# A three-layer CIN kernel: r1 picked from the gathered rows of r0, x ahead of W0 and W1 on the queue, W0's turns behind V2's spreading

## The chip, the cores and the metric

The kernel runs on one core of a Trainium2 chip. The core has a matrix engine (TensorE, PE in the profile, with its weight loads as PEld), a vector engine (VectorE, DVE), a scalar engine (ScalarE, ACT), GpSimd (POOL), a sequencer that only issues transfers (SyncE, SP), and DMA engines that all of these can give work to. Each engine runs its own instructions in the order in which they were written; between engines, semaphores order them. The metric is the time of one launch on the device, in microseconds (us); lower is better.

## The reference

The reference is a compressed interaction network. A sample has 39 fields of 64 numbers; each layer multiplies every row of the layer before with every field, elementwise, and mixes the products into 64 rows:

```python
def _cin_layer(Xk, X0, W, b):
    Wr = W.reshape(O, Hk, Fdim)
    return jnp.einsum('bhe,bfe,ohf->boe', Xk, X0, Wr) + b[None, :, None]
X0 = sparse_embedding            # (1024, 39, 64)
Xk = X0
outs = []
for W, b in ((W0, b0), (W1, b1), (W2, b2)):
    Xk = _cin_layer(Xk, X0, W, b)
    outs.append(Xk.sum(axis=-1))
return jnp.concatenate(outs, axis=-1) @ fc_w.T + fc_b
```

There are 1024 samples and three layers of 64 rows; the result is one number for each sample. All of it is f32.

## The kernel before

**The mathematics.** Only sums of the layers reach the result, so the last layers can be folded into weights: W2 with the last part of fc_w gives a small matrix V2, and W1 with V2 gives a second set of weights beside W0. The kernel then needs, for each column (a sample and one of its 64 places), two quadratic forms of the 39 fields, 64 rows of each. They are one matmul: the products of all pairs of fields, times weights for the 128 rows (wa). One form plus its bias times the other is summed over the 64 places, and the rest is linear.

**Blocks and steps.** The samples are worked in blocks of 32, which are 2048 columns. `load` copies a block's x into a table in DRAM (xd, with a row for each field, and a row of ones written by `fill_ones`). From the table GpSimd gathers rows by lists of row numbers (`roll`, `gather_rows`, L146) into tiles of 128 rows (r0 for the first block, r1 for the second, with five tiles each: rt[0][:, 0] to rt[0][:, 4]). VectorE multiplies two such tiles (`product`, L202): that is a step's product p, 128 pairs by 2048 columns. PE multiplies it with the step's weights (`multiply`, L551), 128 x 512 columns at a time, in two passes for f32, so 8 passes for a step. Four products can be in flight (the pool prods). Six steps and a smaller one (`join`, from the tiles u and v) make the whole of a first block. Later blocks are worked in another form with 32-row pieces (L763), which the change doesn't touch.

**The head.** Before the first step everything has to be made: the lists of rows (small VectorE operations from iotas and constants), a unit matrix, and the weights. The order is that of the code, since the kernel writes each engine's order by hand:

- ScalarE issues the loads of w2s, w0s, x of the first block, and w1s, in this order on one queue; SyncE those of fcrow and the ones.
- PE turns the last part of fc_w into a column, makes V2 from w2s (L378, a VectorE transpose, L419 which spreads it, VectorE's L427), turns W0 (`turn_w0`, L388, seven transposes, which ScalarE copies into the tile both, L479), and multiplies W1 with V2 (`product_v2`, L450). VectorE transposes that (L459), and ScalarE and VectorE copy it into both (`keep_group`, L467 and L470).
- `weight_rows(c)` adds the two halves of both for the pairs of step c (L510, into pairs), `weight_turn(c)` transposes them on PE (L527), and ScalarE copies them to wa (L528, L529).
- The first product needs tiles 0 and 1 of r0. Tile 1 is not waited for: its rows are those of tile 0 in another order. `pick` is a 0/1 matrix with this order, picked its transpose, and four matmuls (L910) pick the rows into four PSUM banks called r1, from which VectorE multiplies (L925). What they pick from is xs: the first block's x, read back from the table by SyncE into 39 rows, with the first 1024 columns at row 0 and the others at row 64 (L243). Its first load waits until w1s has landed.
- `spin` issues matmuls on constants (L261) whose result nobody reads: dummies, 256 columns in two passes each, unless told otherwise. There are some at the start, one behind the pick, five ahead of product_v2, and two and three behind r1, around the first weight turn.

GpSimd issues the gathers of r0 in the order 0, 2, 3, 1, 4, then u and v, then r1's five, then the loads of the second pair of blocks. x of the second block is loaded by SyncE (`load(1, product=...)`), which waits for r0's first gather. Step n's product needs tiles (0, 1), (0, 2), (3, 2), (3, 1), (0, 4), (3, 4) in this order.

Of the kernel before, what the change touches and what calls it, by code (L numbers as in the profile page):

```python
# [16 lines left out]
FT = F + 1  # L17
# [23 lines left out]
NY = 3  # L41
# [73 lines left out]
def cin_kernel(ctx: ExitStack, tc: tile.TileContext, x, w0t, b0, w1, b1, w2, b2, fc_w, fc_b, out):  # L115
# [13 lines left out]
    def bank(name):  # L129
        return psum.tile([128, MM], F32, name=name, tag="po")  # L130
# [14 lines left out]
    def gather_rows(dst, table, k, product=None):  # L145
        work = nc.gpsimd.indirect_dma_start(  # L146
            dst, None, table, bass.IndirectOffsetOnAxis(ap=lists[:, k : k + 1], axis=0)
        )
        behind(work, product)
        return work  # L150
# [37 lines left out]
    xs = ut[1]  # L188
# [19 lines left out]
    with prep as prep:  # L208
# [29 lines left out]
        nc.scalar.dma_start(w2s, w2.rearrange("o (s n) -> (o s) n", s=2))  # L238
        nc.scalar.dma_start(w0s, w0t.rearrange("b (s a) h -> (b s) (a h)", s=NW))
        load(0, nc.scalar)  # L240
        behind_w1 = nc.scalar.dma_start(w1s, w1.rearrange("o (s n) -> (o s) n", s=2))
        for k in range(2):
            work = nc.sync.dma_start(  # L243
                xs[H * k : H * k + F].rearrange("f (k c) -> f k c", c=128),
                xd[0][0:F, bass.ts(k, SUB)].rearrange("f (k c) -> f k c", c=128),
            )
            behind(work, behind_w1)
# [11 lines left out]
        def spin(n=1, cols=MM // 2, to=idle):  # L259
            for _ in range(n):  # L260
                nc.tensor.matmul(  # L261
                    to[:, MM - cols :],
                    nc.const_aps.tensor(1.0, (128, 128), F32),
                    nc.const_aps.tensor(1.0, (128, cols), F32),
                    start=True,
                    stop=True,
                )
# [99 lines left out]
        for h in (0, H):  # L367
            nc.vector.tensor_scalar(pick[:, h : h + F], apart[:, 0:F], seats, None, ALU.is_equal)
        nc.vector.memset(wfin[0:H], 1.0)
        load(1, product=gather_rows(rt[0][:, 0], xd[0][:FT], 0))  # L370
# [41 lines left out]
        for k in range(7):  # L412
            turn_w0(k)
# [71 lines left out]

        for h in (0, H):
            turn_row(h, 1, fcrow, 0)
        turn_row(0, 2, fcrow, 2)
        spin(5)
        for k, a in groups:  # L490
            product_v2(k, a)
# [28 lines left out]
    def weight_turn(c, tr=None):  # L520
        place = len(turned) % 4 * 128
        if place:
            tr = turned[-1]
        elif tr is None:
            tr = bank("tr")
        turned.append(tr)
        nc.tensor.transpose(tr[:, place : place + 128], pairs[:, c], unit)  # L527
        nc.scalar.copy(wa[:, c, 0 : 2 * H], tr[:, place : place + 2 * H])  # L528
        nc.scalar.copy(wa[:, c, 2 * H :], tr[:, place : place + H])  # L529
# [378 lines left out]
    for m in (0, 2, 1, 3):  # L908
        rows = slice(m // 2 * H, m // 2 * H + F)
        nc.tensor.matmul(r1[m], picked[rows], xs[rows, fine[m % 2]], start=True, stop=True)  # L910
    weight_rows(0)
    tr = bank("tr")
    open_block(0)
    spin(2, to=po[0][1])
    weight_turn(0, tr)
    spin(3, to=po[0][1])
# [23 lines left out]
    def whole_step(at, n, c):  # L940
        if at == NPAIR - 1:
            nc.scalar.copy(ones1, ones)
            fill_ones(1, nc.sync, ones1)
            nc.sync.dma_start(b0s, b0.rearrange("(o h) -> o h", o=1).to_broadcast([2, H]))
# [69 lines left out]
    def late_words():  # L1014
        nc.sync.dma_start(b1s, b1.rearrange("(h o) -> h o", o=1).to_broadcast([H, 2]))
        nc.gpsimd.dma_start(b2s, b2.rearrange("(h o) -> h o", o=1))
        nc.gpsimd.dma_start(fcb, fc_b.rearrange("(p o) -> p o", o=1).to_broadcast([NY * 32, 1]))
# [119 lines left out]
```

## Time and profile before

| | |
|---|---|
| median of 3 runs | 738.67 us |
| the runs | 738.67, 741.1, 738.58 us |
| time of the profiled execution | 740.52 us |
| its span, first to last instruction | 738.7 us |
| mean granted PE clock of the span | 0.993 |
| DMA moved | 153.56 MB, mean 208 GB/s |

The profile comes from one execution, which ran by itself and has its own time; times in it count from its first instruction. A row of the timeline gives start and length in us, the engine (with a q for its sequencer, which issues transfers and waits), the line, the operation, the tiles as out<-in, the shapes, how many instructions the row merges, and in brackets how long the engine stood idle before it and what ended that. A row of the chain of waits gives start, length and what the end was waiting for. The granted clock is the share of PE's full clock that was allowed in a stretch.

### The profile page before, as it was taken

Reading aid. Unit: us, or ns where it says so; the run is one execution under the profiler, and the core shown is the slowest. Engines: PE = TensorE matmul, PEld = TensorE weight load, DVE = VectorE, ACT = ScalarE, POOL = GpSimd, SP = SyncE. Lnnn points to the kernel's source line nnn. Section 1 sums busy time; section 2 is a strip of 40 time slices with the busy share of each in tenths; the row PEclk is TensorE's granted clock in tenths of the full one; section 3 lists DMA queues with packets and bytes.
Section 4 is the critical chain, followed back from the end, with each engine's and each line's share of the span. In section 5 each row is a group of like instructions: output and inputs, shape, how many; then the busy total and the mean of one; then the engine's idle time right before and its main releaser. Section 6 shows DMA issues by size and latency. Waiting matters only on the chain.

```text
span 738.7 us, 13824 instructions
## 1 busy us (share of the span) xinstructions
PE 732.6 (99%) x5961; PEld 341.5 (46%) x5961; DVE 636.8 (86%) x566; ACT 114.8 (16%) x199; POOL 522.3 (71%) x287
## 2 busy tenths in 40 slices
PE   8999999999999999999999999999999999999998
PEld 5544444444444444444444444444444444444443
DVE  5979889689797988979889797988979889797996
ACT  3242111020110202011020110202011020200322
POOL 4458887459778697886969778697886869776200
PEclk9899999999999999999999999999999999999999
DMA  7799899752946648284672937548284672855600
GB/s 272 253 333 400 327 275 337 218 177 75 303 140 217 218 124 293 88 279 164 187 273 67 319 119 235 201 133 290 83 294 152 195 261 78 292 188 178 279 0 0
DMA packets 73515, 153.56 MB, mean 208 GB/s; under 512 B 40262, under 2 KB 40347, under 8 KB 69614
## 3 DMA queue, kind: packets, MB, share of 16 engines
q0 software_dynamic: 31936, 131.34, 50.3%
q1 hardware_dynamic: 39833, 19.36, 10.8%
q10 hardware_dynamic: 1685, 1.99, 0.8%
q8 instruction: 46, 0.75, 0.4%
q14 instruction: 15, 0.12, 0.1%
HBM read 150.54 MB, written 10.28 MB: 218 GB/s over the span
## 4 chain that ended last, share of the span: by engine, by line
PE 97%; DMA 2%; ACTq 0%; DVE 0%; ACT 0%; issue 0%; DVEq 0%; SPq 0%
PE po L763 76%; PE po L551 17%; PE po L776 2%; DMA w1s<-in_w 1%; PE po L571 1%; DMA u<-xd 1%; PE po L261 1%; PE r L910 0%; PE po L582 0%; PE idle L910 0%; PE tr L527 0%; ACTq L139 0%; DVE g L827 0%; PE po L691 0%; DVE sums L859 0%; ACT z L825 0%
## 5 line engine op out<-in xcount | busy, mean ns | idle before, releaser
L763 PE MATMUL po<-p,wc 32*128 32x512 f32 x1300 | 561.9, 588 | 0.0
L763 PE MATMUL po<-p,wn 32*128 32x512 f32 x3900 | 561.7, 588 | 0.0
L719 POOL DMA_INDIRECT r<-xd,narrow x130 | 371.9, 2861 | 102.1 <-DVE p L736 69.9
L763 PEld LDWEIGHTS po<-p,wn 32*128 32x128 f32 x3900 | 260.7, 185 | 209.8 <-issue 209.8
L763 PEld LDWEIGHTS po<-p,wc 32*128 32x128 f32 x1300 | 239.4, 185 | 86.6 <-issue 81.7
L736 DVE TENSOR_TENSOR p<-r 128x2048 f32<-128x2048 f32 x78 | 176.1, 2283 | 8.2 <-PE po L763 7.8
L825 ACT ACTIVATE z<-po,columns 64x512 f32<-64x512 f32 x128 | 87.4, 683 | 542.9 <-PE po L763 503.6
L736 DVE TENSOR_TENSOR p<-r,u 128x2048 f32<-128x2048 f32 x52 | 118.6, 2282 | 16.2 <-PE po L763 15.1
L551 PE MATMUL po<-p,wa 128*128 128x512 f32 x288 | 126.2, 596 | 0.0
L202 DVE TENSOR_TENSOR p<-r 128x2048 f32<-128x2048 f32 (+2 forms) x41 | 79.9, 1973 | 10.2 <-PE po L551 9.4
L146 POOL DMA_INDIRECT r<-xd,lists x30 | 65.5, 2183 | 31.1 <-DVE p L736 11.6
L551 PEld LDWEIGHTS po<-p,wa 128*128 128x128 f32 x288 | 54.2, 191 | 68.5 <-issue 61.6
L736 DVE TENSOR_TENSOR p<-r,v 128x2048 f32<-128x2048 f32 x26 | 59.7, 2296 | 25.0 <-PE po L763 25.0
L827 DVE SCALAR_TENSOR_TENSOR g<-po,b0s,z 64x512 f32<-64x512 f32 x76 | 56.9, 749 | 5.8 <-ACT z L825 3.5
L719 POOL DMA_INDIRECT v<-xd,narrow x26 | 37.5, 1444 | 9.1 <-issue 7.6
L827 DVE SCALAR_TENSOR_TENSOR pairs<-po,b0s,z 64x512 f32<-64x512 f32 x26 | 19.5, 749 | 23.9 <-ACT z L825 23.5
L719 POOL DMA_INDIRECT u<-xd,narrow x26 | 28.7, 1103 | 9.5 <-DVE pairs L827 3.4
L809 DVE TENSOR_REDUCE sums<-g 103x16 f32<-103x1024 f32 x26 | 31.3, 1204 | 0.0
L827 DVE SCALAR_TENSOR_TENSOR both<-po,b0s,z 64x512 f32<-64x512 f32 x26 | 19.5, 749 | 0.8
L730 DVE TENSOR_TENSOR p<-u,v 128x1024 f32<-128x1024 f32 x13 | 15.7, 1208 | 1.1 <-PE po L763 1.1
L820 ACT COPY g<-r 39x1024 f32<-39x1024 f32 x12 | 12.1, 1042 | 28.9 <-DVE sums L848 15.6
L809 DVE TENSOR_REDUCE sums<-pairs 103x16 f32<-103x1024 f32 x13 | 15.7, 1205 | 0.0
(161 smaller groups left out, 192.0 us busy)
## 6 DMA issues: line engine op xcount, KB each, us to landing
xd<-in_x SPq DMA_DIRECT2D x27, 312.0 KB
g<-xd SPq DMA_DIRECT2D x26, 156.0 KB
r<-xd,narrow POOLq DMA_INDIRECT x130, 6.3
pairs<-xd SPq DMA_DIRECT2D x13, 156.0 KB
both<-xd SPq DMA_DIRECT2D x13, 156.0 KB
wn<-wc SPq DMA_DIRECT2D x12, 168.0 KB
xd<-in_x POOLq DMA_DIRECT2D x4, 312.0 KB, 8.1
w2s<-in_w ACTq DMA_DIRECT2D x1, 624.0 KB
```

Source lines behind the costliest of these rows:

```text
L146: work = nc.gpsimd.indirect_dma_start(dst, None, table, bass.IndirectOffsetOnAxis(ap=lists[:, k : k + 1], axis=0))
L202: nc.vector.tensor_tensor(p[:, cols], r[:, i, cols], r[:, k, cols], ALU.mult)
L551: nc.tensor.matmul(po[n][m], wa[:, c, side : side + 2 * H], p[:, bass.ts(m, MM)], start=n % 2 == 0 and c == 0, stop=n % 2 == 1 and c == NP ...
L719: work = nc.gpsimd.indirect_dma_start(slot(k, j), None, table, bass.IndirectOffsetOnAxis(ap=narrow[:, j : j + 1], axis=0),)
L730: done = nc.vector.tensor_tensor(p[:, 0:SUB], slot(k, LEFT), slot(k, RIGHT + NK), ALU.mult)
L736: done = nc.vector.tensor_tensor(p.rearrange("p (k c) -> p k c", k=NK), slots(k, many, NK, side), slot(k, one)[:, bass.ts(side, MM)].unsqu ...
L763: nc.tensor.matmul(po[2 * k + side][s], weights(c, s)[:, kind : kind + 2 * H], p[rows, bass.ts(u, MM)], start=begin, stop=last and u == le ...
L776: nc.tensor.matmul(po[2 * k + side][s][half : half + H], weights(LINEAR, s)[:, H : 2 * H], slot(k, NK)[rows, bass.ts(side, MM)], start=Fal ...
L809: nc.vector.tensor_reduce(sums[:, at : at + BB].rearrange("p (h s b) -> p h s b", h=2, s=2)[:, :, side], g[k, side, b].rearrange("p (h b e ...
L820: nc.scalar.copy(gt[H : H + F], tiles_of(n)[0:F, 0, bass.ts(m, SUB)])
L825: nc.scalar.activation(z[one], po[n][m][other], AF.Identity, bias=fc0s[other])
L827: return lambda: nc.vector.scalar_tensor_tensor(gt[0:H, at], po[n][m][one], b0s[one], z[one], ALU.add, ALU.mult)
```

## The change

1. The four r1 matmuls pick from the rows of r0's tile 0 itself, the gathered rows 0 to 38 and 64 to 102, instead of from xs; reading x back into xs goes. Rows 64 to 102 hold the fields in another order (25 to 38, then 0 to 24), so the second half of pick is written in two pieces.
2. On ScalarE's queue x comes ahead of w0s and w1s.
3. The second block's x is loaded by GpSimd, behind the first gather and ahead of the other four, no longer by SyncE with a wait for the gather.
4. W0's turns come behind the spreading of V2 on PE; the three fc turns come behind product_v2.
5. The dummies: one between spreading and W0's turns, two ahead of product_v2, one and a half behind the fc turns; none behind r1. With them go `spin`'s and `weight_turn`'s extra arguments and the early opening of the first block's banks.
6. b0 is loaded in two transfers of 64 rows instead of one; b2 and fc_b by SyncE instead of GpSimd, late in the kernel.

```diff
-        nc.scalar.dma_start(w0s, w0t.rearrange("b (s a) h -> (b s) (a h)", s=NW))
         load(0, nc.scalar)
-        behind_w1 = nc.scalar.dma_start(w1s, w1.rearrange("o (s n) -> (o s) n", s=2))
-        for k in range(2):
-            work = nc.sync.dma_start(
-                xs[H * k : H * k + F].rearrange("f (k c) -> f k c", c=128),
-                xd[0][0:F, bass.ts(k, SUB)].rearrange("f (k c) -> f k c", c=128),
-            )
-            behind(work, behind_w1)
+        nc.scalar.dma_start(w0s, w0t.rearrange("b (s a) h -> (b s) (a h)", s=NW))
+        nc.scalar.dma_start(w1s, w1.rearrange("o (s n) -> (o s) n", s=2))
...
-        for h in (0, H):
-            nc.vector.tensor_scalar(pick[:, h : h + F], apart[:, 0:F], seats, None, ALU.is_equal)
+        for at, f0, n in ((0, 0, F), (H, H % F, F - H % F), (H + F - H % F, 0, H % F)):
+            nc.vector.tensor_scalar(
+                pick[:, at : at + n], apart[:, f0 : f0 + n], seats, None, ALU.is_equal
+            )
...
-        load(1, product=gather_rows(rt[0][:, 0], xd[0][:FT], 0))
+        roll(0, (0,))
+        load(1, nc.gpsimd)
         roll(0, (2, 3, 1, 4))
...
-        for k in range(7):
-            turn_w0(k)
         spread_to = (*pt[:2], pv[1], small)
...
+        spin()
+        for k in range(7):
+            turn_w0(k)
+        spin(2)
+        for k, a in groups:
+            product_v2(k, a)
         for h in (0, H):
             turn_row(h, 1, fcrow, 0)
         turn_row(0, 2, fcrow, 2)
-        spin(5)
-        for k, a in groups:
-            product_v2(k, a)
+        spin()
+        spin(1, MM // 4)
...
     r1 = [idle] + [bank("r1") for _ in range(3)]
-    for m in (0, 2, 1, 3):
-        rows = slice(m // 2 * H, m // 2 * H + F)
-        nc.tensor.matmul(r1[m], picked[rows], xs[rows, fine[m % 2]], start=True, stop=True)
+    for m in range(4):
+        rows = slice(m % 2 * H, m % 2 * H + F)
+        nc.tensor.matmul(r1[m], picked[rows], rt[0][rows, 0, fine[m]], start=True, stop=True)
     weight_rows(0)
-    tr = bank("tr")
-    open_block(0)
-    spin(2, to=po[0][1])
-    weight_turn(0, tr)
-    spin(3, to=po[0][1])
+    weight_turn(0)
...
-            nc.sync.dma_start(b0s, b0.rearrange("(o h) -> o h", o=1).to_broadcast([2, H]))
+            for h in (0, H):
+                nc.sync.dma_start(b0s[h : h + H], b0.rearrange("(h o) -> h o", o=1))
...
-        nc.gpsimd.dma_start(b2s, b2.rearrange("(h o) -> h o", o=1))
-        nc.gpsimd.dma_start(fcb, fc_b.rearrange("(p o) -> p o", o=1).to_broadcast([NY * 32, 1]))
+        nc.sync.dma_start(b2s, b2.rearrange("(h o) -> h o", o=1))
+        nc.sync.dma_start(fcb, fc_b.rearrange("(p o) -> p o", o=1).to_broadcast([NY * 32, 1]))
```

Line numbers move by some lines with this: L910 of before is L908 of the changed kernel, L551 is L549, L450 is L443, L388 is L383, L261 is L253.

What the edits make of PE's order is seen at two places. The first is the head, from the dummy behind the pick to W1's product; idle is the dummies' bank, pw W0's turns, pt and pv the banks of V2 and of W1's product. Before:

```order
L261 MATMUL idle<-const-float32-1.0 128x256
L388 MATMUL pw<-unit,w0s 128x117 x6
L388 MATMUL pw<-unit,w0s 64x117
L419 MATMUL pt<-blocks,twice 64x11 x4
L419 MATMUL pv<-blocks,twice 64x10 x2
L419 MATMUL small<-blocks,twice 64x7 x2
L317 MATMUL small<-ones,fcrow 64x1 x3
L261 MATMUL idle<-const-float32-1.0 128x256 x5
L450 MATMUL pt<-w1s,v_73 128x320 x2
L450 MATMUL pv<-w1s,v_73 128x320 x2
```

PE's order at the same place in the changed kernel, on to the first r1 matmul:

```order
L253 MATMUL idle<-const-float32-1.0 128x256
L412 MATMUL pt<-blocks,twice 64x11 x4
L412 MATMUL pv<-blocks,twice 64x10 x2
L412 MATMUL small<-blocks,twice 64x7 x2
L253 MATMUL idle<-const-float32-1.0 128x256
L383 MATMUL pw<-unit,w0s 128x117 x6
L383 MATMUL pw<-unit,w0s 64x117
L253 MATMUL idle<-const-float32-1.0 128x256 x2
L443 MATMUL pt<-w1s,v_73 128x320 x2
L443 MATMUL pv<-w1s,v_73 128x320 x2
L309 MATMUL small<-ones,fcrow 64x1 x3
L253 MATMUL idle<-const-float32-1.0 128x256
```

W0's turns have moved behind the spreading, three of the five dummies are gone from ahead of W1's product, and the fc turns stand behind it. The second place on PE is from r1 to the first step; r_34x are the r1 banks, po the first block's, tr the turned weights. Before:

```order
L910 MATMUL idle<-u_90,picked 128x512
L910 MATMUL r_342<-u_90,picked 128x512
L910 MATMUL r_341<-u_90,picked 128x512
L910 MATMUL r_343<-u_90,picked 128x512
L261 MATMUL po<-const-float32-1.0 128x256 x2
L527 MATMUL tr<-unit,pairs 128x128
L261 MATMUL po<-const-float32-1.0 128x256 x3
L551 MATMUL po<-p,wa 128x512 x3
```

The same place on PE in the changed kernel:

```order
L908 MATMUL idle<-r_86,picked 128x512
L908 MATMUL r_340<-r_86,picked 128x512
L908 MATMUL r_341<-r_86,picked 128x512
L908 MATMUL r_342<-r_86,picked 128x512
L525 MATMUL tr<-unit,pairs 128x128
L549 MATMUL po<-p,wa 128x512 x3
```

The five dummies are gone, and the operand is the gathered tile r0 (r_86) in place of xs, which lay in the tile u. The third place is GpSimd's queue behind its last constant; r_86 is r0, r_87 the second block's r1, u_89 and v_91 the small tiles, xd_68 the first table. Before:

```order
L332 MEMSET shift_of 128x1 x14
L146 DMA r_86<-xd_68,lists 128x2048 x5
L146 DMA u_89<-xd_68,lists 128x1024
L146 DMA v_91<-xd_68,lists 128x1024
L146 DMA r_87<-xd_68,lists 128x2048 x5
L139 DMA xd_69<-in_x 1248x1x64 x2
```

The same place on GpSimd in the changed kernel:

```order
L324 MEMSET shift_of 128x1 x14
L146 DMA r_86<-xd_68,lists 128x2048
L139 DMA xd_68<-in_x 1248x1x64
L146 DMA r_86<-xd_68,lists 128x2048 x4
L146 DMA u_89<-xd_68,lists 128x1024
L146 DMA v_91<-xd_68,lists 128x1024
L146 DMA r_87<-xd_68,lists 128x2048 x5
L139 DMA xd_69<-in_x 1248x1x64 x2
```

One load stands between the first gather and the other four.

More of the change, by code (lines that the diff above doesn't have):

```diff
@@ L149, in gather_rows @@
         behind(work, product)
-        return work
     def tiles_of(n):
@@ L186, in cin_kernel @@
     vt = [const.tile([128, SUB], F32, name=f"v{k}") for k in range(2)]
-    xs = ut[1]
     ones = const.tile([16, 2, 128], F32, name="ones")
@@ L238, in cin_kernel @@
         nc.scalar.dma_start(w2s, w2.rearrange("o (s n) -> (o s) n", s=2))
+        load(0, nc.scalar)
         nc.scalar.dma_start(w0s, w0t.rearrange("b (s a) h -> (b s) (a h)", s=NW))
-        load(0, nc.scalar)
-        behind_w1 = nc.scalar.dma_start(w1s, w1.rearrange("o (s n) -> (o s) n", s=2))
-        for k in range(2):
-            work = nc.sync.dma_start(
-                xs[H * k : H * k + F].rearrange("f (k c) -> f k c", c=128),
-                xd[0][0:F, bass.ts(k, SUB)].rearrange("f (k c) -> f k c", c=128),
-            )
-            behind(work, behind_w1)
+        nc.scalar.dma_start(w1s, w1.rearrange("o (s n) -> (o s) n", s=2))
         nc.gpsimd.iota(place, pattern=[[0, 1]], base=0, channel_multiplier=1)
@@ L256, in cin_kernel, with spin @@
         idle = bank("idle")
-        def spin(n=1, cols=MM // 2, to=idle):
+        def spin(n=1, cols=MM // 2):
             for _ in range(n):
                 nc.tensor.matmul(
-                    to[:, MM - cols :],
+                    idle[:, 0:cols],
                     nc.const_aps.tensor(1.0, (128, 128), F32),
@@ L518, in cin_kernel, with weight_turn @@
     turned = []
-    def weight_turn(c, tr=None):
+    def weight_turn(c):
         place = len(turned) % 4 * 128
-        if place:
+        if not place:
+            tr = bank("tr")
+        else:
             tr = turned[-1]
-        elif tr is None:
-            tr = bank("tr")
         turned.append(tr)
@@ L907, in cin_kernel @@
     r1 = [idle] + [bank("r1") for _ in range(3)]
-    for m in (0, 2, 1, 3):
-        rows = slice(m // 2 * H, m // 2 * H + F)
-        nc.tensor.matmul(r1[m], picked[rows], xs[rows, fine[m % 2]], start=True, stop=True)
+    for m in range(4):
+        rows = slice(m % 2 * H, m % 2 * H + F)
+        nc.tensor.matmul(r1[m], picked[rows], rt[0][rows, 0, fine[m]], start=True, stop=True)
     weight_rows(0)
-    tr = bank("tr")
-    open_block(0)
-    spin(2, to=po[0][1])
-    weight_turn(0, tr)
-    spin(3, to=po[0][1])
+    weight_turn(0)
     for k, (n, c) in enumerate(steps[:AHEAD]):
```

## The prediction, as it was made before the run

> **What bounds the kernel now.** First the page: engine totals, the granted clock, the chain that ended last.
>
> ```profile
> PE 732.6 (99%) x5961; PEld 341.5 (46%) x5961; DVE 636.8 (86%) x566; ACT 114.8 (16%) x199; POOL 522.3 (71%) x287
> PEclk9899999999999999999999999999999999999999
> PE 97%; DMA 2%; ACTq 0%; DVE 0%; ACT 0%; issue 0%; DVEq 0%; SPq 0%
> ```
>
> TensorE (PE) is 97% of the chain: what it has to multiply is fixed, and only time in which it does nothing useful can go. The change touches only the head of the program, so the second view is the chain of waits over the first 45 us (start, length, what).
>
> ```profile
> 2.86 6.49 DMA w1s<-in_w
> ...
> 9.43 5.36 DMA u<-xd
> ...
> 14.84 1.81 PE idle L910 x2
> 16.65 3.09 PE r L910 x6
> 19.74 2.00 PE po L261 x4
> 21.74 0.21 PE tr L527
> 21.96 2.56 PE po L261 x6
> 24.52 3.07 PE po L551 x6
> 27.59 0.11 PE tr L527
> 27.69 3.44 PE po L551 x8
> ```
>
> The end is set, in order, by the landing of w1s at 9.35, the reading back of xs (u), the four r1 matmuls (L910), the dummies (L261), and from 24.5 the main matmuls (L551) without a break: 3.44 us for a step's 8 passes and 0.11 for a weight turn, a pass of 512 columns being 0.43. The third view gives the granted clock by stretches (the columns after the window: its length, busy time of PE, PEld, DVE, ACT, POOL with counts, clock, DMA share, GB/s).
>
> ```profile
> 13.20:14.80 1.60, 0.00 (x0) 0.00 (x0) 1.44 (x7) 1.24 (x4) 0.94 (x1) 1.00 0.98 218
> 15.43:25.67 10.24, 10.24 (x21) 5.76 (x20) 7.96 (x29) 0.58 (x4) 0.00 (x0) 0.51 0.99 398
> 25.70:40.00 14.30, 14.30 (x38) 6.43 (x37) 12.00 (x41) 3.83 (x12) 10.92 (x6) 1.00 0.62 206
> ```
>
> PE stands still for 1.6 us until u lands, and then runs 10.24 us at half the clock, almost exactly the stretch in which r1, the dummies and the first main passes lie. So the head pays three times: for the wait, for the clock, and for dummies run at that clock.
>
> ```profile
> 24.31 1.06 PE L551 MATMUL po<-p,wa 128*128 128x512 f32 x1
> ```
>
> The main stream starts at 24.31, in the tail of the half clock: its first six passes take 3.07 us of the chain instead of 6 x 0.43 = 2.58. At full clock it would have had to begin at **24.8** to stand where it stands. The working is about how far this point moves.
>
> **The change part by part.** *x ahead of W0, r1 from r0.* The wait of L910 is now for the first gather r0 instead of for u.
>
> ```profile
> 2.00:4.00 2.00, 2.00 (x9) 1.82 (x9) 1.80 (x13) 0.00 (x1) 1.87 (x30) 1.00 0.85 304
> w0s<-in_w0t ACTq DMA_DIRECT2D x1, 380.2 KB
> L146 POOLq EVENT_SEMAPHORE  x1: 43/43/43, 7.2 to 7.2; - x1
> 8.06 1.20 POOL L146 DMA_INDIRECT r<-xd,lists  x1 [3.96 <-DVE v L427]
> 13.90 0.97 SPq L139 DMA_DIRECT2D xd<-in_x  x1
> ```
>
> GpSimd's wait for x ends at 7.2 and the gather starts at 8.06 (the VectorE operation that its row names comes behind that and is none that it reads). SyncE's load of the second block waits for r0 and starts at 13.90, so r0 takes 5.8 us from start to landing. With x ahead, the 380.2 KB of w0s no longer pass before it: 1.2 us at 304 GB/s. r0 then starts at 6.85 and lands at about 12.7. W1 still follows W0 and x on the same queue, so it lands near 9.35 again; r0's data begins behind it. Bounds: 12.3, if nothing of w1s is in its way, to 13.9, if the saving is lost to it; I take 12.7. L908 starts there, 2.1 us before 14.84.
>
> *W0's turns, fewer dummies ahead of W1.* Can PE, VectorE and ScalarE be ready by then?
>
> ```profile
> 6.49 0.86 PE L388 MATMUL pw<-unit,w0s 117*128 117x117 f32 x7
> 8.42 2.44 PE L261 MATMUL idle<-const-float32-1.0 128*128 128x256 f32 x10
> 10.70 1.32 PE L450 MATMUL pt<-w1s,v 128*128 128x320 f32 x4
> 11.86 1.32 PE L450 MATMUL pv<-w1s,v 128*128 128x320 f32 x4
> 11.48 1.09 DVE L459 STREAM_TRANSPOSE flat<-pt 128x320 f32<-128x320 f32 x2 [2.65 <-PE pt L450]
> 7.09 1.93 ACT L479 COPY both<-pw 64x468 f32<-64x468 f32 x4 [0.50 <-PE pw L388]
> 13.77 0.45 DVE L467 COPY both<-flat 64x288 f32<-64x288 f32 x1
> 14.33 0.65 DVE L510 TENSOR_TENSOR pairs<-both 128x4 f32<-128x4 f32 x6
> ```
>
> Five dummies held PE until 10.70 although w1s was there at 9.35. Now two stand ahead of it, and W0's seven turns (0.86 us) run while w1s is awaited: w0s was there by 6.49 and now has x's 312 KB ahead of it, 1.0 us at 304 GB/s, so 7.5 at the latest, and the turns and two dummies end by 9.3. So product_v2 runs 9.4 to 11.9, 1.3 earlier; the three fc turns and two dummies (256 and 128 columns, four passes, 0.65 us) fill PE to about 12.6. VectorE's transposes, the copies and weight_rows(0) follow 1.3 earlier, done at 13.7 instead of 14.98. ScalarE's copies of W0 end near 10 instead of 9.02, ahead of VectorE's first transpose at 10.2, which its next ones need: hidden. One pick operation more is 0.1 to 0.2 us on VectorE before 5.5, hidden behind the wait for w2s and x. Moving b2s and fcb to SyncE and splitting b0s lies hundreds or tens of us from where they are read: zero.
>
> *r1 at full clock.* With PE idle for under half a us ahead of L908 I expect no drop. L910 took 4.90 us at mostly half clock; half of it is 2.45, the low end; 8 passes of 0.43 one after another, 3.44, the high end. I take 2.5, since the row groups alternate as before: done at 15.2, the first bank at 13.7.
>
> *The dummies behind r1.* Four and six passes, 2.00 and 2.56 us, leave the chain. What is late next is the turn of the first weights and ScalarE's two copies of it.
>
> ```profile
> 21.99 0.27 ACT L528 COPY wa<-tr 128x128 f32<-128x128 f32 x1 [7.42 <-PE tr L527]
> 22.16 0.22 ACT L529 COPY wa<-tr 128x64 f32<-128x64 f32 x1
> 18.39 1.28 DVE L925 TENSOR_TENSOR p<-r,r 128x512 f32<-128x512 f32 x2 [1.02 <-PE r L910]
> 20.96 2.42 DVE L202 TENSOR_TENSOR p<-r 128x512 f32<-128x512 f32 x3
> 24.28 2.42 DVE L202 TENSOR_TENSOR p<-r 128x512 f32<-128x512 f32 x3
> 30.63 2.27 DVE L202 TENSOR_TENSOR p<-r 128x2048 f32<-128x2048 f32 x1
> ```
>
> Turn at 15.1, copies done at 15.8 (0.38 from 21.99 to the end of the second), first main matmul at **15.8**. VectorE's quarters run from 13.75, one each 0.64: the first is ready at 14.4. Does VectorE keep ahead? Its spacing in these rows is p1 2.57 behind the second quarter, p2 3.32 later, p4 6.35 after p2. So p1 starts at 16.9, p2 at 20.2, p4 at 26.6, done at 28.9; PE's fifth step, four times 3.55 after 15.8, wants p4 at 30.0. It holds, with 1.1 us to spare where there were 6.1 before (32.9 against 24.8 and the same 14.2): the lead that hid VectorE is nearly spent, and from there it grows again.
>
> *The second block's x by GpSimd.* This is what can spend the rest.
>
> ```profile
> 9.56 0.94 POOL L146 DMA_INDIRECT r<-xd,lists  x1 [0.30 <-issue]
> 27.30 0.94 POOL L146 DMA_INDIRECT u<-xd,lists  x1 [13.07 <-DVE p L202]
> 41.00 2.07 POOL L139 DMA_DIRECT2D xd<-in_x  x2
> xd<-in_x POOLq DMA_DIRECT2D x2, 312.0 KB, 9.7
> ```
>
> Issuing a load on GpSimd takes 1.0 us (2.07 for two), with 0.3 of gap. r0 ends its issue at 8.05, so the next gather issues at 9.4 instead of 9.56: not later. Its data, 312 KB, now stands ahead of r2's in the same queue, 0.8 us at the 398 GB/s above; a gather's megabyte is 2.6 us. r2 lands near 16.1, r3 18.7, tile 1 21.3, tile 4 24.0, against needs of 16.9, 20.2, 23.5 and 26.6. u's gather, held until 27.30 because SyncE's load lands late, is free at 14.4; the gathers behind it move up by as much, so nothing later starves. What the load costs is bounded by nothing and by its 9.7 us to landing; I take 0.8, from the rate.
>
> The Trainium skill speaks against this step: "DMA: Bandwidth & Descriptors", section "Issuing engine by pattern", gives simple loads to Sync and calls that path generally faster. The trace does not agree here: GpSimd's loads land 9.7 after issue under load, SyncE's kept u waiting over 13. By the rule the second rival below would be likelier.
>
> **The sum**, against the profiled execution: L908 starts 2.1 earlier; r1 takes 2.4 less; the dummies' 4.56 go and 0.5 of waiting comes, 4.0; the first passes at full clock, 0.5. Together 9.0, or 24.8 to 15.8. That execution took 740.52 (span 738.7), so **731.5**. It took 1.85 longer than the median of the runs shown, 738.67; I take that for the half-clock stretch, which need not cost the same in each execution, and since I expect none, I count from the profiled one. Counted from the median it would be 729.7. I say 731.6.
>
> **The rivals.** *The clock drops all the same.* L910 uses 39 of 128 rows, and PE stayed at half clock right through it; if such matmuls count as little work, L908 and the 0.5 us wait behind it look like the gap of before, and the dummies that followed are gone. A stretch of 10.24 at half clock behind 15.8 costs 5.1: 736.6; if dense matmuls end it after a third, 733.2. For it speaks the row at 15.43; against it, that PE has no standstill of 1.6 us any more.
>
> The Trainium skill, "TensorE: Matmul & The Clock Gate", section "Why this matters for your kernels", asks only that no idle gap exceed about 3 us; here 1.6 us was enough, so the measurement decides. By its rule neither kernel would drop, and the new time would be the forecast. Its Part 1 says that the activity window is 3413 ns and free-running; three of them are the 10.24 seen here, which the trace bears out, and its phase would differ between executions.
>
> *The load ahead of r2 costs its worst.* If it lands 8 us after issue, at 16.2, then r2 lands at 19, p1 is 2.4 late and p4 1.4 behind PE: 733.0. The long times to landing speak for it, but those were taken with other gathers in the queue.
>
> *r0 does not land earlier*, because W0 and W1 now run beside it: L908 at 13.9, 1.2 lost, 732.8. So the reordering would not do what it says; the rest would.
>
> *Slower.* The clock drops twice in a row: ScalarE's copies, VectorE's thin lead and the missing dummies leave holes in the first steps, and every hold of 10.24 brings the next. Each costs 5.1, so from the second on, 10.2 exceeds the 9.0 won: 741.7. Against it: from 25.7 the trace shows not one drop in a stream of the same steps.
>
> **How the numbers follow.** Forecast 0.56; clock drop 0.26; load ahead of r2 0.08; r0 not earlier 0.06; slower 0.04. The range reaches from the count from the median, with L908 at its early end (729.2), to the full drop (736.8); only the slower rival and odd phases lie outside. About 0.5% is what a measurement of this kernel can tell from no change: 735.0 to 742.4 is then "the same". The forecast, the load, r0 and a third of the clock drop lie below 735.0, 0.78; the rest of the drop and part of the slower rival are the same, 0.19; 0.03 are above.
>
> **What would show it.** Right: L908 at 12.7 directly behind the dummies, a granted clock of 1.00 through 10 to 30, first main matmul near 15.8, no PE idle before p4. Wrong: a clock near 0.5 anywhere between 12 and 26; VectorE's p1 released by the gather of r; L443 released by w1s well after 9.4; any PE idle in the first five steps.

## The result, and the profile after

The changed kernel took 732.50 us (median of 6 runs, 732.12 to 733.14), the kernel before 738.66 (median of 6, 738.57 to 741.1): a ratio of 0.991, interval 0.9895 to 0.9923. The forecast was 731.6, with a range of 729.2 to 736.8. The profiled execution of the changed kernel took 732.4, its span 730.6. On another chip its median was 736.84 against 739.34 (e11 below).

The page of the changed kernel, engine totals, granted clock and shares of the chain:

```profile
PE 725.8 (99%) x5951; PEld 336.7 (46%) x5951; DVE 636.7 (87%) x567; ACT 114.9 (16%) x199; POOL 528.1 (72%) x286
PEclk9999999999999999999999999999999999999999
PE 98%; DMA 1%; ACTq 0%; DVE 0%; ACT 0%; issue 0%; DVEq 0%
```

PE is busy for 6.8 us less than the 732.6 of before, and the one slice with an 8 in its clock is gone. The chain of waits over the changed kernel's first 45 us (start, length, what):

```profile
2.66 6.04 DMA w0s<-in_w0t
...
8.74 0.92 PE pw L383 x7
9.66 0.88 PE idle L253 x4
10.54 1.23 PE pt L443 x4
11.77 1.16 PE pv L443 x4
...
14.10 0.62 PE idle L908
...
15.15 0.86 PE r L908 x5
16.01 0.27 PE tr L525
16.31 0.28 ACT wa L526
...
16.63 2.84 PE po L549 x6
```

The end is no longer set by w1s and u but by w0s, which lands at 8.69, three us later than the 5.69 of before; from there PE works almost without a break, at full clock, until the main stream starts at 16.63 instead of 24.31. VectorE's products in the timeline of the changed kernel (in brackets the idle time before a row and what ended it):

```profile
18.60 2.43 DVE L200 TENSOR_TENSOR p<-r 128x512 f32<-128x512 f32 x3 [0.16 <-DMA r<-xd,lists]
...
28.23 2.28 DVE L200 TENSOR_TENSOR p<-r 128x2048 f32<-128x2048 f32 x1
...
35.23 2.27 DVE L200 TENSOR_TENSOR p<-r 128x2048 f32<-128x2048 f32 x1
```

The last row is the second block's first product. Before, the same product came behind a wait (timeline of VectorE, kernel before):

```profile
41.76 2.29 DVE L202 TENSOR_TENSOR p<-r 128x2048 f32<-128x2048 f32 x1 [4.06 <-PE po L551]
```

The row names PE, but the second block's tile 1 landed at 41.57: this product waited for its data. GpSimd's gathers tell why it no longer does (timeline of GpSimd, changed kernel):

```profile
7.43 1.18 POOL L146 DMA_INDIRECT r<-xd,lists  x1 [3.54 <-DVE blocks L404]
8.62 1.07 POOL L139 DMA_DIRECT2D xd<-in_x  x1
...
16.87 0.94 POOL L146 DMA_INDIRECT u<-xd,lists  x1 [2.13 <-DVE p L919]
```

The gather of u starts at 16.87 where it started at 27.30, and what is queued behind it comes earlier too: the second block's tile 1 lands at 33.55 instead of 41.57.

For all that follows a span is cut in three: from the start to the first main matmul, from there to the first matmul of the part stage (the 32-row form of the later blocks), and from there to the end. In the two profiled executions:

| kernel | first main matmul at | main to part | part to end | span |
|---|---|---|---|---|
| before | 24.31 | 90.49 | 623.93 | 738.7 |
| changed | 16.63 | 90.06 | 623.93 | 730.6 |

The whole difference of 8.1 lies ahead of the first main matmul (7.68) and in the tail of the half clock behind it (0.43). The medians differ by 6.2 only, because the profiled execution of before was 1.85 above its median.

### The profile page after: what moved, and what is told of

It is laid out like the page before. It is cut to its first block, busy times and chain, and to the rows that moved or that the text cites. A ratio compares the mean times of both kernels' runs of the same rounds, so it can differ in the third digit from the quotient of the medians.

```text
span 730.6 us, 13801 instructions
## 1 busy us (share of the span) xinstructions
PE 725.8 (99%) x5951; PEld 336.7 (46%) x5951; DVE 636.7 (87%) x567; ACT 114.9 (16%) x199; POOL 528.1 (72%) x286
## 4 chain that ended last, share of the span: by engine, by line
PE 98%; DMA 1%; ACTq 0%; DVE 0%; ACT 0%; issue 0%; DVEq 0%
PE po L761 77%; PE po L549 17%; PE po L774 2%; DMA w0s<-in_w0t 1%; PE po L569 1%; PE po L580 0%; PE idle L253 0%; ACTq L139 0%; PE pt L443 0%; PE pv L443 0%; PE tr L525 0%; PE idle L908 0%; PE pw L383 0%; PE r L908 0%; DVE g L825 0%; PE po L689 0%
## 5 line engine op out<-in xcount | busy, mean ns | idle before, releaser
L549 PE MATMUL po<-p,wa 128*128 128x512 f32 x288 | 125.8, 594 | 0.4 <-ACT wa L526 0.4
L146 POOL DMA_INDIRECT r<-xd,lists x30 | 70.2, 2338 | 31.4 <-DVE p L734 11.6
L549 PEld LDWEIGHTS po<-p,wa 128*128 128x128 f32 x288 | 53.7, 190 | 68.6 <-issue 62.0
L825 DVE SCALAR_TENSOR_TENSOR pairs<-po,b0s,z 64x512 f32<-64x512 f32 x26 | 19.5, 749 | 23.9 <-ACT z L823 23.5
L825 DVE SCALAR_TENSOR_TENSOR both<-po,b0s,z 64x512 f32<-64x512 f32 x26 | 19.5, 749 | 0.8
L807 DVE TENSOR_REDUCE sums<-both 103x16 f32<-103x1024 f32 x13 | 15.7, 1205 | 0.0
```

The lines of the kernel that those rows point to most:

```text
L146: work = nc.gpsimd.indirect_dma_start(dst, None, table, bass.IndirectOffsetOnAxis(ap=lists[:, k : k + 1], axis=0))
L549: nc.tensor.matmul(po[n][m], wa[:, c, side : side + 2 * H], p[:, bass.ts(m, MM)], start=n % 2 == 0 and c == 0, stop=n % 2 == 1 and c == NP ...
L807: nc.vector.tensor_reduce(sums[:, at : at + BB].rearrange("p (h s b) -> p h s b", h=2, s=2)[:, :, side], g[k, side, b].rearrange("p (h b e ...
L825: return lambda: nc.vector.scalar_tensor_tensor(gt[0:H, at], po[n][m][one], b0s[one], z[one], ALU.add, ALU.mult)
```

## The experiments

The first four ran together on one chip, with 29 runs of the kernel before beside them (median 739.48); the next four (before: 738.97) and the last four (before: 739.34) on another. Each head below names the kernel that was edited; the lines with + and - are the edit.

**e1: the kernel before, its gap filled.** Does the half clock carry the loss?

```diff
         for k, a in groups:
             product_v2(k, a)
+        spin(4)
```

> The kernel before, with four dummies (8 passes, about 1.75 us) behind product_v2, where PE stood still until u landed; nothing else. Theory (the standstill of 1.6 us takes the clock): the granted clock stays 1.00 from 7 us on, the r1 matmuls take 2.0 to 2.5 us in place of 4.9, the ten dummy passes behind them 2.2 in place of 4.6, the first main matmul starts at 19.5 to 20.5 in place of 24.3, and the time falls by 2.5 to 4.5 us to 734.2 to 736.2. Rival (matmuls of 39 rows count as idle and take the clock themselves): the clock drops to 0.50 for 10.24 us all the same and the time stays at 738 to 740.

Measured: 741.1 (738.22 to 743.99, 12 runs), ratio 1.0015 [0.9999, 1.0031]. Its rows of PE's timeline, and its clock by stretches (length; busy time and counts of PE, PEld, DVE, ACT, POOL; clock; DMA share; GB/s):

```profile
16.50 1.95 PE L911 MATMUL r<-u,picked 39*128 39x512 f32 x6 [0.71 <-DMA u<-xd]
70.19 19.12 PE L552 MATMUL po<-p,wa 128*128 128x512 f32 x44 [1.96 <-DVE p L202]
```

```profile
18.57:21.99 3.42, 3.42 (x9) 2.64 (x9) 3.42 (x13) 0.58 (x4) 0.00 (x0) 0.50 1.00 413
```

The clock part came in part: not full clock, as the theory had it, but 3.4 us at half clock instead of 10.24, behind the 0.71 that PE still waited for u. The main stream began at 22.45 (its first matmul), 1.9 earlier, where 19.5 to 20.5 was expected. The time did not follow: PE then stood for 1.96 at 68.2, for the second block's products, and the part stage lost 1.4 more. So an earlier head alone buys nothing. Neither theory had that.

**e2: the kernel before, without the dummies behind r1.**

```diff
-    spin(2, to=po[0][1])
     weight_turn(0, tr)
-    spin(3, to=po[0][1])
```

> The kernel before without the five dummies behind r1; nothing else. Theory as the prediction added it up (each term by itself): the 4.6 us of dummies less 0.5 of waiting leave the head, time 734.6. Rival (the half-clock stretch is of fixed length, so main passes take the dummies' place in it at half speed): the first main matmul starts near 20.3, but the stretch runs on to 25.4, and the gain is half of what the stretch still holds, 1.5 to 2.5 us: 736.2 to 737.2.

Measured: 739.73 (739.08 to 743.87, 12), ratio 1.0007 [0.9993, 1.0022]: none of the gain. The first main matmul came at 18.40, 5.9 earlier than before, but main to part took 94.18 instead of 90.49, and part to end 625.77 instead of 623.93. The chains of waits show where it went, first e2's, then the changed kernel's:

```profile
18.40 5.38 PE po L551 x6
...
112.66 12.34 PE po L763 x96
```

```profile
106.76 10.51 PE po L761 x96
```

Some of it is the half clock, as this run's rival had it: the stretch ran from 16.71 to 23.54, now under main passes, and the first six took 5.38 where they had taken 3.07 before. PE then waited 0.8 in two places for VectorE at the second block's products, and the first 96 matmuls of the part stage took 1.83 longer than in the changed kernel, at full clock; what slows these isn't shown. So about 2 of the 5.9 went to the clock, and the rest was given back behind it.

**e3: the changed kernel with the old order of the loads** (W0 ahead of x).

```diff
+        nc.scalar.dma_start(w0s, w0t.rearrange("b (s a) h -> (b s) (a h)", s=NW))
         load(0, nc.scalar)
-        nc.scalar.dma_start(w0s, w0t.rearrange("b (s a) h -> (b s) (a h)", s=NW))
```

> The changed kernel with w0s ahead of x again on ScalarE's queue; nothing else. Theory as predicted (r0's landing sets r1, x ahead of W0 is worth 1.2 us): L908 starts 0.6 to 1.2 later, 733.1 to 733.7. Rival (PE sets it: W1's landing, its product and the dummies behind it): w0s lands near 5.7 and w1s near 9.4, PE is ready for L908 by 13.3, r0 lands near 13.9, L908 starts at 13.9 to 14.1 as now, and the time is within 0.3 of 732.5.

Measured: 732.07 (731.93 to 733.65, 5), ratio 0.9902 [0.9886, 0.9917]. From its chain of waits:

```profile
7.57 0.36 DVE v L420 x3
...
7.98 5.45 DMA r<-xd,lists
13.43 0.04 issue
13.47 0.69 PE idle L908
```

r0 landed at 13.43; with x ahead it landed at 13.40. In this pair x's place on the queue moves nothing at r0. (Over all the traces r0 landed from 12.47 to 15.14 with x ahead and from 13.34 to 15.33 with W0 ahead, so a small gain would not be seen.) With W0 first PE's work ahead of r1 is done in time, so that L908 starts at 13.47 instead of 14.03, which neither the theory nor the rival had.

**e4: the changed kernel with the second block's x by SyncE,** as before.

```diff
-        roll(0, (0,))
-        load(1, nc.gpsimd)
+        load(1, product=gather_rows(rt[0][:, 0], xd[0][:FT], 0))
```

> The changed kernel with the second block's x loaded by SyncE behind the landing of r0's first gather, as before; nothing else. Theory as predicted (the load costs r2 under 1 us that PE doesn't feel, and otherwise changes nothing that PE waits for): r2 lands 1 to 2 us earlier, p1 starts near 18, time within 0.3 of 732.5. Rival (the load by SyncE lands near 26, holds GpSimd's gather of u and with it the second block's tiles): u is gathered at 27 in place of 16.9, the second block's first product waits for its tile until 40 or later in place of 35.2, PE stands idle 1 to 4 us at 41 and the time is 733.5 to 736.5.

Measured: 739.45 (737.34 to 740.61, 12), ratio 0.9997 [0.9987, 1.0008]. The whole gain is gone with this one edit. VectorE's second block and PE's waits in its timeline:

```profile
43.49 2.29 DVE L201 TENSOR_TENSOR p<-r 128x2048 f32<-128x2048 f32 x1 [5.99 <-DMA r<-xd,lists]
```

```profile
15.19 0.69 PE L908 MATMUL idle<-r,picked 39*128 39x512 f32 x1 [0.54 <-DMA r<-xd,lists]
17.86 4.54 PE L549 MATMUL po<-p,wa 128*128 128x512 f32 x6 [0.36 <-ACT wa L526]
45.83 3.70 PE L549 MATMUL po<-p,wa 128*128 128x512 f32 x8 [1.88 <-DVE lane_of L596]
49.70 17.53 PE L549 MATMUL po<-p,wa 128*128 128x512 f32 x40 [0.17 <-DVE p L201]
68.00 19.12 PE L549 MATMUL po<-p,wa 128*128 128x512 f32 x44 [0.77 <-DVE p L201]
```

The load, issued at 15.16, sent its first data at 19.6 and its last at 26.0; u's gather started at 27.09; the second block's first product at 43.49, 8.3 later than in the changed kernel. PE waits 2.82 for it in three places, the first 96 matmuls of the part stage take 1.37 more, and a stretch of 3.4 at half clock behind the 0.54 at L908 costs some 1.7. The main stream also began 1.2 later than in the changed kernel, since r0 landed at 15.14 in this execution. So of the 8.2 between the two spans about 2.9 are the head and the clock. The one run of e4 with a mean clock of 0.999 took 737.34, 4.8 above the changed kernel; that is nearer to what the late second block costs by itself. The rival of this run was right in kind; its worst was 4.

**e5: the kernel before with only that edit,** the second block's x by GpSimd.

```diff
-        load(1, product=gather_rows(rt[0][:, 0], xd[0][:FT], 0))
+        roll(0, (0,))
+        load(1, nc.gpsimd)
```

> The kernel before with the second block's x loaded by GpSimd behind r0's first gather, and nothing else of the change. Theory (two walls: PE's head and the tiles of the second block; either alone holds the end): PE's head is as before, with the standstill and the half clock, u is gathered near 18 in place of 27, VectorE's wait ahead of the second block's first product goes, and the time stays within 1 us of before, 738.5 to 740. Rival (the second block's tiles alone set the end): the time falls to 733 to 736.

Measured: 735.83 (734.94 to 739.07, 10), ratio 0.996 [0.9943, 0.9977]: about half the gain, with the old head. The theory of two walls that each hold the end by themselves missed; the number lies in the rival's range. Its gather of u (timeline of GpSimd):

```profile
17.24 0.94 POOL L146 DMA_INDIRECT u<-xd,lists  x1 [1.94 <-DMA xd<-in_x]
```

Main to part takes 90.15 here, although its profiled execution had 6.8 us of half clock, nearly all of it ahead of the main stream. That execution's span is only 1.5 below the span of before. The four runs with a mean clock of 0.999 or more have spans of 733.1 to 733.8, so most of the gain comes from executions in which the clock drops little.

**e6: dummies behind r1 in the changed kernel.** They write into the bank of the first r1 matmul, so the first quarter of the first product is made from the dummies' result instead of the picked rows, and waits for them.

```diff
+    spin(2)
     weight_turn(0)
+    spin(3)
```

> The changed kernel with five dummies put back behind r1, two ahead of the first weight turn and three behind it, into the bank idle; nothing else. Theory (at full clock the ten passes cost 0.22 each, less the half us of waiting that they fill): first main matmul 1.7 to 2.2 later than 16.6, time 734.0 to 734.7. As the prediction priced them (4.56 at half clock): 736.5 or more. Rival (VectorE sets the start anyway): within 0.3 of 732.5.

Measured: 736.24 (734.98 to 742.07, 12), ratio 0.9972 [0.9954, 0.999]. Since VectorE is made to wait for the dummies, this doesn't price them; e10 does.

**e7: the changed kernel without the one and a half dummies ahead of r1.**

```diff
-        spin()
-        spin(1, MM // 4)
```

> The changed kernel without the one and a half dummies that stand between the fc turns and the r1 matmuls; nothing else. Theory (PE, not r0's landing at 13.40, held L908 until 14.03): L908 at 13.45, first main matmul at 16.1, clock stays 1.00, time 731.9 to 732.2. Rival (without them the stretch around r1 holds too little work and the clock drops as in the kernel before): a stretch at 0.50 of 3.4 to 10.2 us behind 13.7, time 733.5 to 737.

Measured: 733.81 (732.95 to 734.59, 6), ratio 0.9933 [0.9916, 0.9949]. The timeline of PE:

```profile
9.79 1.62 PE L383 MATMUL pw<-unit,w0s 117*128 117x117 f32 x7 [1.90 <-DMA w0s<-in_w0t]
```

A drop came, from 9.35 to 12.76, but not where the dummies had been: PE stood for 1.90 ahead of W0's turns, because w0s landed at 9.74. This run says little on the dummies and a lot on W0.

**e8: the kernel before with three edits,** GpSimd's load, the filled gap, and no dummies behind r1; it still reads x back into xs.

```diff
-        load(1, product=gather_rows(rt[0][:, 0], xd[0][:FT], 0))
+        roll(0, (0,))
+        load(1, nc.gpsimd)
...
+        spin(4)
...
-    spin(2, to=po[0][1])
     weight_turn(0, tr)
-    spin(3, to=po[0][1])
```

> The kernel before with three edits: the second block's x by GpSimd, four dummies behind product_v2, none behind r1. r1 is still picked from x read back, in the old order of loads. Theory (the second wall gone, what is left is the head): u lands at 14.8 to 16.4, r1 ends at 17 to 18.5, first main matmul at 17.6 to 19, time 733.5 to 735.5, so that picking from r0 itself is worth 1 to 3 us. Rival (the clock drops as it did with the gap filled, and PE pays half of 3.4 to 10.2 us more): 735.5 to 739.

Measured: 734.34 (733.63 to 736.36, 6), ratio 0.9948 [0.993, 0.9966], as expected. Full clock throughout, first main matmul at 18.05, main to part 90.06. From its chain of waits:

```profile
14.88 1.05 PE idle L912 x2
15.93 1.50 PE r L912 x6
...
18.05 2.84 PE po L553 x6
```

So what is left of the change, picking from r0's rows with the head's new order, is worth the rest: 18.05 against 16.63 for the changed kernel, 1.4 by the profiled executions. The medians don't settle it: e8 is 1.8 above the changed kernel's first runs, and 2.5 below its runs on e8's own chip (e11).

**e9: the changed kernel without its dummies behind V2's spreading.**

```diff
-        spin()
         for k in range(7):
             turn_w0(k)
-        spin(2)
         for k, a in groups:
             product_v2(k, a)
...
-        spin()
-        spin(1, MM // 4)
```

> The changed kernel without any of its dummies behind V2's spreading: not the one ahead of W0's turns, the two ahead of W1's product, nor the one and a half ahead of r1; nothing else. Theory (the dummies hold the clock): with PE idle about 1.2 us ahead of W0's turns and 0.6 ahead of W1's product, the clock drops for 3.4 to 10.2 us in most executions, and the median is 1.5 to 4 us above that of the changed kernel in this call. Rival (without an idle gap of 3 us nothing drops): the clock stays 1.00, L908 starts at 13.45, and the time is 0 to 0.6 us below the changed kernel's.

Measured: 737.38 (732.86 to 738.73, 9), ratio 0.9941 [0.9914, 0.9968]. In its profiled execution the clock dropped from 11.19 to 14.60, behind a standstill of 1.98 ahead of W0's turns, and again from 18.01 to 24.84. All nine runs have a mean clock of 0.997 or less, while six of the twelve of e11, which has the dummies, have 0.998 or more: the dummies do hold the clock in part of the executions. The median is only 0.5 above e11's, since half of e11's runs lost as much, so neither the theory's time nor the rival's clock came. The timeline has something else, PE first, ScalarE second:

```profile
16.78 0.33 PE L521 MATMUL tr<-unit,pairs 128*128 128x128 f32 x1
20.18 1.22 PE L545 MATMUL po<-p,wa 128*128 128x512 f32 x1 [3.07 <-ACT wa L522]
```

```profile
19.86 0.27 ACT L522 COPY wa<-tr 128x128 f32<-128x128 f32 x1 [3.88 <-remote]
```

The turn of the first weights starts at 16.78, and ScalarE may copy it only at 19.86; in the changed kernel this takes 0.37 (15.94 to 16.31). Neither engine shows work in between. The trace's semaphore records show that the count by which PE reports the turn came at 19.84, though the turn's row ends at 17.11; in the changed kernel it came 0.02 behind the row's end, at 16.29. A like hole, 6.1 long, is in the profiled execution of e10 (its turn ends at 19.74, the copy starts at 25.82), and one of 2.1 in that of e6, there between PE's last dummy (to 18.73) and VectorE's first product (20.87).

**e10: the changed kernel with the five dummies behind r1 as before,** in a bank of the first block's.

```diff
+    tr = bank("tr")
+    open_block(0)
+    spin(2, to=po[0][1])
-    weight_turn(0)
+    weight_turn(0, tr)
+    spin(3, to=po[0][1])
```

> The changed kernel with the five dummies behind r1 put back as they stood before, two ahead of the first weight turn and three behind it, into the first block's second bank; nothing else. Theory (at full clock the ten passes cost 0.22 each, less what they fill of the wait for the copies): first main matmul 1.5 to 2.2 us later than in the changed kernel, and the time as much above it. As the prediction priced them (4.56, at half clock): 4 us above. Rival (VectorE sets the start anyway): within 0.4.

**e11: the changed kernel again; e12: e3 again,** on the same chip and beside it.

> The changed kernel as it is, as the measure for the others of this call. All theories: 732.0 to 733.5, granted clock of the span 0.998 to 1.000 in all but a few executions.

> The changed kernel with w0s ahead of x again, as once before. Theory (x's place on the queue is worth nothing or less, since r0's data then shares the DMA engines with W0 and W1, and W0 lands late): 0.2 to 0.8 us below the changed kernel of this call. Rival (the difference seen was that of two chips): within 0.2, or above it.

| kernel | median, range (runs) | ratio to before |
|---|---|---|
| e10, dummies back | 736.08, 733.82 to 744.44 (12) | 0.9955 [0.9927, 0.9982] |
| e11, changed kernel | 736.84, 732.68 to 740.95 (12) | 0.9962 [0.9935, 0.9989] |
| e12, old load order | 732.58, 732.14 to 733.85 (6) | 0.9900 [0.9874, 0.9926] |

The changed kernel did not keep to its 732.0 to 733.5. It has two groups of runs on this chip: six from 732.68 to 735.07 with a mean granted clock of 0.998 or more, six from 738.62 to 740.95 with 0.992 to 0.995. Its profiled execution is one of the first group, and shows the start of it (PE's timeline, then the clock by stretches):

```profile
9.69 1.63 PE L383 MATMUL pw<-unit,w0s 117*128 117x117 f32 x7 [1.78 <-DMA w0s<-in_w0t]
```

```profile
9.54:12.95 3.41, 3.26 (x12) 2.88 (x13) 0.00 (x0) 1.88 (x4) 2.50 (x4) 0.50 0.92 339
```

W0 landed at 9.64 here, not 8.69, PE stood for 1.78, and the clock dropped. With W0 first (e12) there is no such wait: its turns start at 7.73, and PE's only standstill above half a us is the one for r0, without a drop:

```profile
13.88 0.69 PE L908 MATMUL idle<-r,picked 39*128 39x512 f32 x1 [0.76 <-DMA r<-xd,lists]
```

e12 beats both kernels in one and the same set of runs, the changed one by 4.3 us in the medians, far more than its theory had; by the runs with a mean clock of 0.999 or more it is 0.85 (732.41 against 733.26), about what the theory had. The rest is that none of e12's six runs is in the upper group, where six of e11's twelve are. For the dummies, the runs with a mean clock of 0.999 or more compare: five of e10 lie from 733.82 to 734.87 and one at 737.4, three of e11 from 732.68 to 734.19, five of e12 from 732.14 to 733.2. So they cost about 1 us at full clock, by the medians of e10 and e11 (e12 has the other load order).

## Why the prediction was right, and where not

The three kinds of evidence, as one table (profiled executions; u is the start of its gather):

| kernel | u | first main | main to part | part to end | span |
|---|---|---|---|---|---|
| before | 27.30 | 24.31 | 90.49 | 623.93 | 738.7 |
| e1 | 28.63 | 22.45 | 92.83 | 625.30 | 740.6 |
| e2 | 27.09 | 18.40 | 94.18 | 625.77 | 738.4 |
| e4 | 27.09 | 17.86 | 95.24 | 625.73 | 738.8 |
| e5 | 17.24 | 23.12 | 90.15 | 624.01 | 737.3 |
| e8 | 17.04 | 18.05 | 90.06 | 624.03 | 732.1 |
| e3 | 16.19 | 16.15 | 90.06 | 623.93 | 730.1 |
| changed | 16.87 | 16.63 | 90.06 | 623.93 | 730.6 |

Where u is gathered near 27, a main stream that starts earlier takes longer, and the spans stay at 738.4 to 740.6 whatever the head does. (Of what is lost behind the first main matmul, the half clock takes 2.5 in e2 and 1.7 in e4; the rest, 3.4 and 5.3 against the changed kernel, is the second block and the start of the part stage.) Where u is gathered near 17, the rest is constant and each us of the head is a us of the span.

**The sum was right, its account was not.** The prediction put the gain at the head: "L908 starts 2.1 earlier; r1 takes 2.4 less; the dummies' 4.56 go and 0.5 of waiting comes, 4.0; the first passes at full clock, 0.5. Together 9.0". From 24.8 to the measured 16.63 it is 8.2, and those 0.8 are nearly all of the 0.9 between 731.6 and 732.5. Term by term, from the two chains: L908 started 0.8 earlier and not 2.1 (14.03 for 14.84), r1 took 2.9 less and not 2.4, the dummies with the wait gave 3.95 for 4.0, the first passes 0.43 for 0.5. So one term failed by 1.3, and that half a us of it was made up by another is luck.

**The step that failed most is the second block's x.** The prediction entered it as a cost: "What the load costs is bounded by nothing and by its 9.7 us to landing; I take 0.8". It did see that u "is free at 14.4; the gathers behind it move up by as much, so nothing later starves", but gave this no value and did not ask what would starve without it. By the runs the step is what lets the head count: taken back, it returns all of the gain in the median (e4), some 5 of it by the second block and the rest by the clock and a late r0; the head's gains without it are nothing (e1, e2); alone it gives 3.1 (e5). The row that would have told it is VectorE's 4.06 of idle at 41.76, in the trace of before: PE did not wait there only because it came late itself. Put 8 us forward, PE would have waited.

The same omission is in how the prediction counted. It set the 1.85 between the profiled execution and the median down to the half clock, "which need not cost the same in each execution". The runs of before bear that out by half: in the three sets, 15 runs with a mean clock of 0.993 or 0.994 (10 us at half clock) have spans of 737.2 to 740.0, median 739.0; 13 without a drop (1.00) have 736.0 to 738.1 and one 740.6, median 736.7. A whole drop costs some 5 us at the head by the prediction's count, but only 2.3 of them came out. That the second wall stood right behind the first is borne out by e5, where it is gone: there the two runs at 0.995 (about 7 us at half clock) have spans 3.5 above those of the four at 0.999 or more, while the ten of before at 0.995 are only 1.7 above the 13 without a drop.

**"r0 then starts at 6.85 and lands at about 12.7": wrong.** GpSimd's gather started at 7.43, and r0 landed at 13.40. x landed at 6.53, 0.6 earlier than the 7.17 of before and not 1.2, since x's packets now took 2.5 us (3.6 to 6.1) where they had taken 1.7 (5.1 to 6.8). What was left was lost between start and landing: in e3, with W0 first, they are 7.98 and 13.43. This is the rival "r0 does not land earlier", which had 0.06 and gave 732.8; 732.5 was measured. The other price of this part, w0s at "7.5 at the latest", was the worse error: W0 landed at 8.69, since its packets (5.0 to 7.9) no longer had the queue to themselves but ran beside W1's (5.2 to 9.5). W1, forecast "near 9.35 again", landed at 10.24, and PE's weight load for L443 waited for it (10.34), so L443 would have been late even with W0 in time. L443 started at 10.54 in the chain, not 9.4, and L908 at 14.03 was released by PE's own work, not by r0. In the six other traces with x ahead W0 came at 8.99 to 9.82, and in four of them the clock dropped there (e7, e9, e10, e11). Two of the prediction's own signs of being wrong came true, then, L443 held by w1s and p1 released by a gather (below), in a result inside the range.

**r1 at full clock: 2.5 expected, 1.98 measured** (14.03 to 16.01). It fell short of the low end of 2.45.

**The dummies behind r1: mis-sized.** Their 4.56 were at half clock; at full clock e10 prices them at about 1. In the prediction's sum this did no harm, because the half clock went too, and the remainder was counted under the dummies.

**VectorE's lead.** p1 started at 18.60, released by the gather of r2, not at 16.9: r2 landed at 18.58 where 16.1 was forecast. p4 ended at 30.51, and PE's fifth step began at 30.91 without a gap: 0.4 to spare where 1.1 had been given. The rival of the load ahead of r2 described this lateness (r2 at 19) correctly; PE's own start, 0.8 late, took it up.

**The clock.** No drop in the changed kernel's first runs, as forecast. Of the reason given, "PE has no standstill of 1.6 us any more", the runs confirm the rule and not the kernel: with standstills of 1.78 to 1.98 ahead of W0's turns the clock dropped (e7, e9, e10, e11), with 0.55 to 1.36 there it did not (changed kernel, e6, e4). The rival of a drop had looked for it at r1; in these it comes at W0's turns. At r1 it came in e4, where r0 landed late, and in the kernels that pick from xs (e1, e2, e5), behind waits of 0.46 to 0.78.

**The Trainium skill's rule on who issues loads** ("DMA: Bandwidth & Descriptors", section "Issuing engine by pattern": simple loads by Sync, that path being generally faster) was not put to the test. Here the same 312 KB by SyncE, behind r0, held u until 27.09 (e4), and by GpSimd until 16.87. But of these 10.2 us 6.5 lie in the issue, since SyncE's load waited for r0 (issued at 15.16 against 8.62), and 3.7 in the time from issue to landing (11.2 against 7.5). A load by SyncE without that wait was not run. The prediction's "over 13" for SyncE mixes the two as well: from its issue at 13.90 that load took 12.7.

**Open.** The hole between the turn of the first weights and its copy in e9 and e10, and behind the last dummy in e6, isn't explained: the engines' rows show nothing in it, and PE's report is late without a cause that the trace names. It may be what holds back the upper six runs of e11, since one 3.4-us stretch at half clock (the profiled run, 735.07) doesn't account for 739 to 741; those runs have no trace, so this wasn't shown.

## What to carry to other kernels

When a head is shortened, ask of each stage behind it how much its data was early: an engine's idle time that cost nothing (here VectorE's 4.06 at 41.76) says how much of the gain the next wall will take. Price what lets later data start earlier at what it would cost to take it back, not at the packets that it puts in the way. And a queue's order is judged by every landing on it: bringing x forward by 0.6 us moved r0 by next to nothing, W0 back by 3 and W1 by 0.9.

## What the runs showed of the hardware

- **A standstill of PE far below 3 us can halve the clock, and not each does.** In the 3.41 us ahead of a drop PE had stood idle for 1.49 (e7), 1.63 (e11), 1.64 (e10), 1.66 (before), 1.85 (e9), and 2.16 (e10) and 2.28 (e6) in the holes named above. In stretches of 3.41 on the same grid, counted back from each trace's drop, 1.14 (e6) and 1.36 (e4) brought none. Where r1's matmuls on 39 rows lay in the stretch, 0.46 (e2), 0.71 (e1), 0.78 (e5), 0.89 (e4) and 0.91 (e9, its second) were enough, while 0.36 (changed kernel) and 0.76 (e12) were not, on the grid that the clock's first rise gives. No run was made to find the limit. The drops last whole multiples of 3.41: 3.41 (e1, e4, e7, e11, the first of e9 and of e10), 6.83 (e2, e5, e6, the second of e9 and of e10), 10.24 (before). The Trainium skill, "TensorE: Matmul & The Clock Gate", gives a free-running window of 3413 ns (Part 1), which these lengths bear out, and asks in "Why this matters for your kernels" only for no gap above about 3 us, which they do not.
- **The same load is cut differently by who issues it.** The second block's x, 312 KB from DRAM to DRAM, went out as 1248 packets of 256 bytes when SyncE issued it (19.6 to 26.0 in e4, 4.4 after its issue, beside the gathers), and as 78 packets of 4096 bytes when GpSimd did (12.2 to 15.5 in the changed kernel).
- **A load on a queue also shares the DMA engines with the load issued behind it.** With x first, W0's and W1's packets ran side by side from 5.2 on, and W0 landed between 8.69 and 9.82 in different executions; with W0 first its packets were through by 5.1 and it landed at 5.63 (e3).
